# A gated-scan block: softmax of the gates spread over ScalarE, VectorE and GpSimd, with the scan states in PSUM

## The chip, the cores and the metric

The kernel runs on one core of one Trainium2 chip. The metric is the device time of one launch in microseconds; several runs of the same kernel are taken and their median is given. A core has TensorE (PE, matrix products[...]), VectorE (DVE), ScalarE (ACT), GpSimd (POOL) and the DMA queues that SyncE (SP) and ACT issue to. Each engine works through its own instructions in a fixed order and waits on semaphores for the others.

## The reference

One block works on x of shape 8 x 512 x 128 (batch, time, width), all in fp32. The part around the change is the attention half: a softmax over 17 values for each of 8 x 16 rows of each token, and a recurrence over time with these gates.

```python
h = _rmsnorm(x, norm_w)
v = (h @ W_v.T).reshape(B, T, H, M)                       # H = 8, M = 16
gate_logits = (h @ W_a.T).reshape(B, T, H, M, M + 1)
gates = jax.nn.softmax(gate_logits, axis=-1)
a0 = gates[..., 0]
A = gates[..., 1:]
A_t = jnp.moveaxis(A, 1, 0)
u_t = jnp.moveaxis(a0 * v, 1, 0)

def step(state, inp):
    At, ut = inp
    new = jnp.einsum('bhij,bhj->bhi', At, state) + ut
    return (new, new)
...
return x + h_out @ W_out.T
```

Before it stands a layernorm with modulation; after it a second one, a router that keeps 4 of 8 experts, and all 8 experts (128 to 256 gated, and back to 128) with their weighted sum.

## The kernel before

Tokens are taken in tiles of 128: 16 time steps of 8 batches. There are 32 tiles, and four of them make a superchunk. The scan is serial over all 32 tiles. The work is written as Python generators that yield where other work may come between; beside the scan of tile c run the output of the attention of tile c - 1 (`attn_out`), the gates of tile c + 2 (`gates`), and a quarter of the experts of the superchunk before (`experts`), with the first layernorm (`ln1`) or the second one and the router (`attn_post`) where they fall due. From this the framework makes the fixed order of each engine and all semaphores. The timeline shows that the order on an engine isn't simply the order of the text: pieces of two tiles' gates, scan steps and expert work are mixed, and the experts of a whole superchunk come in one stretch.

`gates(c)` (L203 to L248): ACT scales the normalised tokens, PE transposes them into a buffer of `ps_misc` (ph, L209), ACT copies them out (hnT, L211). PE then makes the 2176 logits of each token in five pieces, one PSUM bank each (pg, L220), in a pool of two banks; the last bank also holds v. For each piece DVE takes the maxima over 17 values (mx, L224) and subtracts them (ee, L226), and ACT takes the exponential (L229). Over the whole tile DVE then sums (z, L234), inverts (L235), scales (L238) and multiplies gate 0 by v (L241). Eight DMAs on SP's queue (L243) bring the tile from tokens-by-partition to g, which has the 64 pairs of head and batch on its partitions and time within them.

`scan(c)` (L250 to L262): for each of 16 time steps DVE multiplies the gates by the previous state (L256) and reduces over 17 values to the new state (L259), which lies in ys.

`attn_out(c)` (L264 to L282): eight DMAs on SP's queue bring ys back to tokens (yt, L269); PE transposes (py, L273), ACT copies (ytT, L275), PE multiplies by the output weights (po, L277), and DVE adds h (r, L281). py, po and ph, and the matrices of the second layernorm, the router and the experts' biases, all use buffers of `ps_misc`, of which there are two:

```python
ps_gate = ctx.enter_context(tc.tile_pool(name="ps_gate", bufs=2, space=PS))
ps_gu = ctx.enter_context(tc.tile_pool(name="ps_gu", bufs=3, space=PS))
ps_dn = ctx.enter_context(tc.tile_pool(name="ps_dn", bufs=1, space=PS))
ps_misc = ctx.enter_context(tc.tile_pool(name="ps_misc", bufs=2, space=PS))
```

The second layernorm's and router's lines are L287, L288, L174, L178, L179 and L320 to L329 on DVE. In the experts DVE's lines are L382 to L384 on the activations and L399 on the weighted sum; ACT's are L371, L373 and L375.

Of the kernel before, what the change touches and what calls it, by code (L numbers as in the profile page):

```python
# [9 lines left out]
F32 = mybir.dt.float32  # L10
AF = mybir.ActivationFunctionType
ALU = mybir.AluOpType
AX = mybir.AxisListType

P = 128
# [13 lines left out]
def adaln_block_kernel(  # L29
    ctx: ExitStack,  # L30
    tc: tile.TileContext,
    x: bass.AP,        # [B, T, D]
    norm_w: bass.AP,   # [D, 1]
    wa_t: bass.AP,     # [D, H*M*(M+1)]
    wv_t: bass.AP,     # [D, D]
    wo_t: bass.AP,     # [D, D]
    rw_t: bass.AP,     # [D, E]
    r_bias: bass.AP,   # [1, E]
    gu_t: bass.AP,     # [D, E*2I]
    gu_bias: bass.AP,  # [128, E*4]  # L40
    dn_t: bass.AP,     # [E, I, D]
    dn_bias: bass.AP,  # [E, D]
    c_in: bass.AP,     # [B, D]
    w_mod: bass.AP,    # [D, 6*D]
    out: bass.AP,      # [B, T, D]
):
    nc = tc.nc
    B, T, D = x.shape
    H, M = 8, 16
    J = M + 1               # softmax width  # L50
    NG = H * M              # softmax groups per token
    TT = P // B             # time steps in a tile of 128 tokens
    NT = T // TT            # tiles
    KT = 4                  # tiles in a superchunk
    NS = NT // KT
    E = rw_t.shape[1]
    I = dn_t.shape[1]
    IC = I // P
    NW = KT * P
    # (first softmax group, groups) of each PSUM bank; v goes into the last bank  # L60
    CHUNKS = [(0, 27), (27, 27), (54, 26), (80, 26), (106, 22)]

    const = ctx.enter_context(tc.tile_pool(name="const", bufs=1))
# [2 lines left out]
    scan_p = ctx.enter_context(tc.tile_pool(name="scan", bufs=3))  # L66
    ffn_p = ctx.enter_context(tc.tile_pool(name="ffn", bufs=3))
    small = ctx.enter_context(tc.tile_pool(name="small", bufs=2))
    PS = bass.MemoryType.PSUM
    ps_gate = ctx.enter_context(tc.tile_pool(name="ps_gate", bufs=2, space=PS))  # L70
    ps_gu = ctx.enter_context(tc.tile_pool(name="ps_gu", bufs=3, space=PS))
    ps_dn = ctx.enter_context(tc.tile_pool(name="ps_dn", bufs=1, space=PS))
    ps_misc = ctx.enter_context(tc.tile_pool(name="ps_misc", bufs=2, space=PS))

    def misc_psum(name):
        return ps_misc.tile([P, 512], F32, tag="misc", name=name)

# [1 line left out]
    c_sb = const.tile([B, D], F32, name="c_sb")  # L79
    nc.sync.dma_start(c_sb, c_in)  # L80
    wmod_sb = const.tile([P, 6 * D], F32, name="wmod_sb")
    nc.scalar.dma_start(wmod_sb, w_mod)
    x_sb = const.tile([P, NT, D], F32, name="x_sb")

    def load_x(c):
        nc.sync.dma_start(x_sb[:, c, :], x[:, c * TT : (c + 1) * TT, :])

    for c in range(KT):
        load_x(c)
    wav = const.tile([P, NG * J + D], F32, name="wav")  # L90
    nc.scalar.dma_start(wav[:, : NG * J], wa_t)
    nc.scalar.dma_start(wav[:, NG * J :], wv_t)
    nw_sb = const.tile([P, 1], F32, name="nw_sb")
    nc.sync.dma_start(nw_sb, norm_w)
    wo_sb = const.tile([P, D], F32, name="wo_sb")
    nc.sync.dma_start(wo_sb, wo_t)
    for c in range(KT, NT):
        load_x(c)
# [10 lines left out]
    dn_sb = const.tile([P, E * IC, D], F32, name="dn_sb")  # L109
    nc.scalar.dma_start(dn_sb, dn_t.rearrange("e (ic p) d -> p (e ic) d", p=P))  # L110

# [1 line left out]
    ident = const.tile([P, P], F32, name="ident")  # L113
    make_identity(nc, ident)
    eps_sb = const.tile([P, 1], F32, name="eps_sb")
    nc.gpsimd.memset(eps_sb, EPS)
    state0 = const.tile([H * B, M], F32, name="state0")
    nc.gpsimd.memset(state0, 0.0)
    # lower[e, f] = 1 where f < e: among equal logits the lower index goes first
    lower = const.tile([P, E, E], F32, name="lower")  # L120
    nc.gpsimd.memset(lower, 1.0)
    nc.gpsimd.affine_select(
        out=lower, in_=lower, compare_op=ALU.is_gt, fill=0.0, base=0,
        pattern=[[1, E], [-1, E]], channel_multiplier=0,
    )
    # up's bias with the 1 of (up + 1)
    ub1_sb = const.tile([P, E, IC], F32, name="ub1_sb")
    nc.vector.tensor_scalar(ub1_sb, gub_sb[:, :, IC:], 1.0, None, ALU.add)

# [1 line left out]
    sig_c = const.tile([B, D], F32, name="sig_c")  # L131
    nc.scalar.activation(sig_c, c_sb, AF.Sigmoid)
    sil = const.tile([B, D], F32, name="sil")
# [2 lines left out]
    nc.tensor.transpose(psil[:, :B], sil, ident[:B, :B])  # L136
    silT = const.tile([P, B, TT], F32, name="silT")
    nc.vector.tensor_copy(silT, psil[:, :B].unsqueeze(2).to_broadcast([P, B, TT]))
    mod = const.tile([P, 6, D], F32, name="mod")
# [18 lines left out]
    def mod_row(i):  # L158
        return mod[:, i, :].unsqueeze(1).to_broadcast([P, KT, D])

# [1 line left out]
    def layernorm(dst, src, scale_i, shift_i, tag):  # L162
        mv = small.tile([P, KT, 2], F32, tag="mv" + tag, name="mv" + tag)
        for k in range(KT):
# [13 lines left out]
        nc.vector.tensor_tensor(dst, dst, mod_row(scale_i), ALU.mult)  # L178
        nc.vector.tensor_tensor(dst, dst, mod_row(shift_i), ALU.add)  # L179

    # the parts below are generators: they yield where other work may come between
    h_tiles = {}      # superchunk -> (h, rms factor)
    g_tiles = {}      # tile -> gates for the scan
    y_tiles = {}      # tile -> scan states
    r_tiles = {}      # superchunk -> h + attention
    f_tiles = {}      # superchunk -> what the experts need

    def ln1(s):
        h = sc_p.tile([P, KT, D], F32, tag="h", name=f"h{s}", bufs=3)
# [13 lines left out]
    def gates(c):  # L203
        h, rr = h_tiles[c // KT]
        k = c % KT
        hn = tile_p.tile([P, D], F32, tag="hn", name=f"hn{c}")
        nc.scalar.activation(hn, h[:, k, :], AF.Copy, scale=rr[:, k : k + 1])
        ph = misc_psum(f"ph{c}")
        nc.tensor.transpose(ph[:, :P], hn, ident)  # L209
        hnT = tile_p.tile([P, P], F32, tag="hnT", name=f"hnT{c}")  # L210
        nc.scalar.activation(hnT, ph[:, :P], AF.Copy, scale=nw_sb)  # L211
        ee = tile_p.tile([P, NG, J], F32, tag="ee", name=f"ee{c}")
        mx = tile_p.tile([P, NG], F32, tag="mx", name=f"mx{c}")
        v = tile_p.tile([P, NG], F32, tag="v", name=f"v{c}")
        yield
        for g0, n in CHUNKS:
            last = g0 + n == NG
            w = n * J + (D if last else 0)
            pg = ps_gate.tile([P, 512], F32, tag="pg", name=f"pg{c}_{g0}")
            nc.tensor.matmul(  # L220
                pg[:, :w], hnT, wav[:, g0 * J : g0 * J + w], start=True, stop=True
            )
            pg3 = pg[:, : n * J].rearrange("p (g j) -> p g j", j=J)
            nc.vector.tensor_reduce(mx[:, g0 : g0 + n], pg3, AX.X, ALU.max)  # L224
            e3 = ee[:, g0 : g0 + n, :]
            nc.vector.tensor_tensor(  # L226
                e3, pg3, mx[:, g0 : g0 + n].unsqueeze(2).to_broadcast([P, n, J]), ALU.subtract
            )
            nc.scalar.activation(e3, e3, AF.Exp)  # L229
            if last:  # L230
                nc.scalar.copy(v, pg[:, n * J : w])
            yield
        z = tile_p.tile([P, NG], F32, tag="z", name=f"z{c}")
        nc.vector.tensor_reduce(z, ee, AX.X, ALU.add)  # L234
        nc.vector.reciprocal(z, z)  # L235
        yield
        g = scan_p.tile([H * B, TT, M, J], F32, tag="g", name=f"g{c}")
        nc.vector.tensor_tensor(  # L238
            ee, ee, z.unsqueeze(2).to_broadcast([P, NG, J]), ALU.mult
        )  # L240
        nc.vector.tensor_tensor(ee[:, :, 0], ee[:, :, 0], v, ALU.mult)  # L241
        for hh in range(H):
            nc.sync.dma_start(  # L243
                g[hh * B : (hh + 1) * B].rearrange("b t i j -> b t (i j)"),
                ee[:, hh * M : (hh + 1) * M, :].rearrange("p i j -> p (i j)"),
            )
        g_tiles[c] = g
        yield  # L248

    def scan(c):  # L250
        g = g_tiles.pop(c)
        ys = scan_p.tile([H * B, TT, M], F32, tag="ys", name=f"ys{c}")
        prev = state0 if c == 0 else y_tiles[c - 1][:, TT - 1, :]
        for t in range(TT):
            a = g[:, t, :, 1:]
            nc.vector.tensor_tensor(  # L256
                a, a, prev.unsqueeze(1).to_broadcast([H * B, M, M]), ALU.mult
            )
            nc.vector.tensor_reduce(ys[:, t, :], g[:, t, :, :], AX.X, ALU.add)  # L259
            prev = ys[:, t, :]  # L260
            yield
        y_tiles[c] = ys  # L262

    def attn_out(c):  # L264
        s, k = c // KT, c % KT
# [18 lines left out]
    def attn_post(s):  # L284
# [9 lines left out]
        h2T = sc_p.tile([P, NW], F32, tag="h2T", name=f"h2T_{s}")  # L294
        nc.scalar.copy(h2T, ph)
        yield
        # router: top 4 of 8, softmax over the chosen
        pr = misc_psum(f"pr{s}")
        for k in range(KT):
            nc.tensor.matmul(  # L300
# [16 lines left out]
        other = lg.unsqueeze(2).to_broadcast([P, KT, E, E])  # L317
# [21 lines left out]
            comb, comb, cs.unsqueeze(2).to_broadcast([P, KT, E]), ALU.mult  # L339
        )  # L340
        yield
        # the experts' output biases, weighted
        pc = misc_psum(f"pc{s}")
        for k in range(KT):
            nc.tensor.transpose(pc[:E, k * P : (k + 1) * P], comb[:, k, :], ident)
# [13 lines left out]
    def experts(s, es):  # L359
# [18 lines left out]
        def back(e, ic, gt, up, sg):  # L378
            if ic == 0:
                acts[e] = ffn_p.tile([P, IC, NW], F32, tag="act", name=f"act{s}_{e}", bufs=2)  # L380
            # clip(up, -7, 7) + 1, min(gate, 7), sigmoid(1.702 min(gate, 7))
            nc.vector.tensor_scalar(up, up, 1.0 - LIMIT, 1.0 + LIMIT, ALU.max, ALU.min)  # L382
            nc.vector.scalar_tensor_tensor(up, gt, LIMIT, up, ALU.min, ALU.mult)  # L383
            nc.vector.scalar_tensor_tensor(acts[e][:, ic, :], sg, SIG_MAX, up, ALU.min, ALU.mult)  # L384
# [50 lines left out]
        for _ in gen:  # L435
            pass

    # ---- the pipeline: beside the scan of tile c run the gates of tile c + 2,
    # the output of tile c - 1 and a part of the experts of the superchunk before
    run(ln1(0))  # L440
    run(gates(0))
    run(gates(1))
    for c in range(NT):
        s, k = c // KT, c % KT
        beside = []
# [12 lines left out]
        other = chain(*beside)  # L458
# [3 lines left out]
        run(other)  # L462
    run(attn_out(NT - 1))
    run(attn_post(NS - 1))
# [42 lines left out]
```

## Time and profile before

| | |
|---|---|
| median of 3 runs | 1391.12 us (1390.35 to 1391.66) |
| profiled execution: its span, the only time that its page gives | 1390.6 us |
| VectorE busy | 1151.2 us, 83% |
| TensorE matmuls busy | 675.7 us, 49% |
| ScalarE busy | 462.8 us, 33% |
| GpSimd busy | 1.1 us |
| DMA g<-ee | 256 DMAs of 136 KB on SP's queue |
| DMA yt<-ys | 256 DMAs of 8 KB on SP's queue |

In a row of a group stand the line, the engine, the operation, what is written from what, the shapes and the count; then busy time in us and the mean of one in ns; then the engine's idle time just before these instructions and what ended most of it. In a timeline a row begins with its start and its length in us, and an idle time before it stands in brackets with what ended it. In a table by stage a row begins with the stretch and its length, followed by the busy us (and count of instructions) of PE, PE's weight loads, DVE, ACT and POOL, the granted TensorE clock, the DMA engines' busy share and GB/s. Work that overlaps is counted once in an engine's busy time.

### The profile page before, as it was taken

How to read it: one execution, taken by the hardware profiler on the slowest of the kernel's cores; microseconds unless marked ns; L12 is line 12 of the kernel's file. 1: busy time of each engine (PE TensorE's matmuls, PEld its weight loads, DVE VectorE, ACT ScalarE, POOL GpSimd, SP SyncE). 2: the span in 40 equal slices, each digit the busy share in tenths (PEclk: the TensorE clock that was granted, in tenths of full speed). 3: DMA queues.
4: the chain of work that ended last, by engine and by line, in shares of the span. 5: the costliest groups of instructions: out<-in, count | busy, mean ns of one | idle time of the engine just before them, and what ended most of it. 6: DMA issues, size and time to landing. Idle time of an engine off the chain costs nothing.

```text
span 1390.6 us, 9491 instructions
## 1 busy us (share of the span) xinstructions
PE 675.7 (49%) x2181; PEld 348.3 (25%) x2181; DVE 1151.2 (83%) x2533; ACT 462.8 (33%) x850; POOL 1.1 (0%) x10
## 2 busy tenths in 40 slices
PE   1415049531594237830496315942369414771077
PEld 0101015310262014510153102620135201440044
DVE  3889699996999799996989969897898978888366
ACT  2401037320382115610373203821146102541054
POOL 0000000000000000000000000000000000000000
PEclk9755568865697667965688656976569756795579
DMA  6251514024330325005140242303241041501200
GB/s 199 32 60 14 60 21 49 1 32 45 36 31 10 44 25 65 2 11 63 20 51 0 30 48 33 34 10 38 31 50 17 10 54 20 61 1 21 24 0 8
DMA packets 80248, 47.39 MB, mean 34 GB/s; under 512 B 38064, under 2 KB 79296, under 8 KB 79936
## 3 DMA queue, kind: packets, MB, share of 16 engines
q1 hardware_dynamic: 78640, 42.03, 25.8%
q10 hardware_dynamic: 1552, 4.75, 1.0%
q14 instruction: 38, 0.31, 0.1%
q8 instruction: 18, 0.29, 0.1%
HBM read 6.91 MB, written 2.10 MB: 6 GB/s over the span
## 4 chain that ended last, share of the span: by engine, by line
DVE 40%; PE 32%; DMA 21%; issue 2%; SPq 2%; ACT 2%; DVEq 0%; ACTq 0%
DMA g<-ee 15%; PE pgt L365 9%; PE pd L391 8%; DVE g L256 8%; PE pup L367 8%; DVE ys L259 7%; DVE mx L224 5%; DVE z L234 5%; DMA yt<-ys 4%; PE pg L220 4%; DVE ee L226 4%; DVE ee L238 3%; SPq L243 2%; DVE z L235 2%; DMA x_sb<-in_x_dram 1%
## 5 line engine op out<-in xcount | busy, mean ns | idle before, releaser
L256 DVE TENSOR_TENSOR g<-g,ys 64x256 f32<-64x256 f32 x511 | 211.2, 413 | 107.0 <-DMA g<-ee 60.1
L220 PE MATMUL pg<-wav,hnT 128*128 128x459 f32 (+2 forms) x320 | 221.6, 815 | 133.5 <-DVE ee L226 108.7
L259 DVE TENSOR_REDUCE ys<-g 64x16 f32<-64x272 f32 x512 | 217.1, 424 | 11.3
L273 PE MATMUL py<-ident,yt 128*128 128x128 f32 x32 | 13.7, 427 | 436.5 <-DMA yt<-ys 435.8
L275 ACT COPY ytT<-py 128x128 f32<-128x128 f32 x32 | 8.5, 266 | 513.1 <-PE py L273 513.1
L391 PE MATMUL pd<-dn_sb,act 128*128 128x128 f32 x1024 | 146.6, 291 | 29.8 <-DVE act L384 16.2
L391 PEld LDWEIGHTS pd<-dn_sb,act 128*128 128x128 f32 x1024 | 136.2, 201 | 91.3 <-DVE act L384 36.6
L229 ACT ACTIVATE ee<-ee 128x459 f32<-128x459 f32 (+2 forms) x160 | 89.1, 564 | 201.4 <-DVE ee L226 179.6
L365 PE MATMUL pgt<-h2T,gu_sb 128*128 128x512 f32 x256 | 145.9, 654 | 0.0
L367 PE MATMUL pup<-h2T,gu_sb 128*128 128x512 f32 x256 | 138.8, 625 | 0.0
L220 PEld LDWEIGHTS pg<-wav,hnT 128*128 128x128 f32 x320 | 68.9, 254 | 257.2 <-issue 163.1
L273 PEld LDWEIGHTS py<-ident,yt 128*128 128x128 f32 x32 | 6.2, 193 | 461.3 <-issue 302.2
L224 DVE TENSOR_REDUCE mx<-pg 128x27 f32<-128x459 f32 (+2 forms) x160 | 95.1, 594 | 13.5 <-PE pg L220 12.8
L373 ACT ACTIVATE up<-pup,ub_sb 128x512 f32<-128x512 f32 x128 | 86.8, 678 | 40.8 <-PE pup L367 40.8
L371 ACT ACTIVATE gate<-pgt,gub_sb 128x512 f32<-128x512 f32 x128 | 87.6, 684 | 24.7 <-PE pgt L365 24.2
L226 DVE TENSOR_TENSOR ee<-pg,mx 128x459 f32<-128x459 f32 (+2 forms) x160 | 95.2, 595 | 0.0
L384 DVE SCALAR_TENSOR_TENSOR act<-sg,up 128x512 f32<-128x512 f32 x128 | 88.1, 688 | 7.4 <-ACT sg L375 3.4
L383 DVE SCALAR_TENSOR_TENSOR up<-gate,up 128x512 f32<-128x512 f32 x128 | 88.0, 688 | 2.9
L399 DVE SCALAR_TENSOR_TENSOR y<-pd,comb,y 128x128 f32<-128x128 f32 x256 | 74.9, 342 | 14.2 <-PE pd L391 13.9
L375 ACT ACTIVATE sg<-gate 128x512 f32<-128x512 f32 x128 | 80.5, 629 | 2.5
L234 DVE TENSOR_REDUCE z<-ee 128x128 f32<-128x2176 f32 x32 | 76.8, 2400 | 0.5 <-ACT ee L229 0.5
L238 DVE TENSOR_TENSOR ee<-ee,z 128x2176 f32<-128x2176 f32 x32 | 76.9, 2404 | 0.0
(89 smaller groups left out, 599.1 us busy)
## 6 DMA issues: line engine op xcount, KB each, us to landing
g<-ee SPq DMA_DIRECT2D x256, 136.0 KB
yt<-ys SPq DMA_DIRECT2D x256, 8.0 KB
x_sb<-in_x_dram SPq DMA_DIRECT2D x32, 64.0 KB
gu_sb<-in_gu_t_dram ACTq DMA_DIRECT2D x1, 2048.0 KB
out_dram<-y SPq DMA_DIRECT2D x32, 64.0 KB
wav<-in_wa_t_dram ACTq DMA_DIRECT2D x1, 1088.0 KB
wmod_sb<-in_w_mod_dram ACTq DMA_DIRECT2D x1, 384.0 KB
wo_sb<-in_wo_t_dram SPq DMA_DIRECT2D x1, 64.0 KB
```

The costliest lines, as they stand in the source:

```text
L220: nc.tensor.matmul(pg[:, :w], hnT, wav[:, g0 * J : g0 * J + w], start=True, stop=True)
L224: nc.vector.tensor_reduce(mx[:, g0 : g0 + n], pg3, AX.X, ALU.max)
L226: nc.vector.tensor_tensor(e3, pg3, mx[:, g0 : g0 + n].unsqueeze(2).to_broadcast([P, n, J]), ALU.subtract)
L229: nc.scalar.activation(e3, e3, AF.Exp)
L234: nc.vector.tensor_reduce(z, ee, AX.X, ALU.add)
L238: nc.vector.tensor_tensor(ee, ee, z.unsqueeze(2).to_broadcast([P, NG, J]), ALU.mult)
L256: nc.vector.tensor_tensor(a, a, prev.unsqueeze(1).to_broadcast([H * B, M, M]), ALU.mult)
L259: nc.vector.tensor_reduce(ys[:, t, :], g[:, t, :, :], AX.X, ALU.add)
L365: nc.tensor.matmul(pgt, gu_sb[:, e, ic * P : (ic + 1) * P], h2T, start=True, stop=True)
L367: nc.tensor.matmul(pup, gu_sb[:, e, I + ic * P : I + (ic + 1) * P], h2T, start=True, stop=True)
L384: nc.vector.scalar_tensor_tensor(acts[e][:, ic, :], sg, SIG_MAX, up, ALU.min, ALU.mult)
L391: nc.tensor.matmul(pd[:, k, :], act[:, ic, k * P : (k + 1) * P], dn_sb[:, e * IC + ic, :], start=(ic == 0), stop=(ic == IC - 1),)
```

## The change

The logits of all five banks are copied to SBUF by ACT. DVE takes the maxima of the whole tile in one instruction, GpSimd subtracts them, ACT takes one exponential of the whole tile, DVE sums and inverts as before, and GpSimd scales and multiplies gate 0 by v. The scan writes its states into one PSUM bank, yp, in two halves that tiles use in turn, and reads the previous state from there; after a tile's scan ACT copies its states to SBUF, from where the DMAs take them as before. The bank comes from `ps_misc`, which keeps one buffer. Comments that the diff drops are left out here.

```diff
-    ps_misc = ctx.enter_context(tc.tile_pool(name="ps_misc", bufs=2, space=PS))
+    ps_misc = ctx.enter_context(tc.tile_pool(name="ps_misc", bufs=1, space=PS))
+    ps_y = ctx.enter_context(tc.tile_pool(name="ps_y", bufs=1, space=PS))
...
+    yp = ps_y.tile([H * B, 2, TT, M], F32, name="yp")
...
             pg3 = pg[:, : n * J].rearrange("p (g j) -> p g j", j=J)
-            nc.vector.tensor_reduce(mx[:, g0 : g0 + n], pg3, AX.X, ALU.max)
-            e3 = ee[:, g0 : g0 + n, :]
-            nc.vector.tensor_tensor(
-                e3, pg3, mx[:, g0 : g0 + n].unsqueeze(2).to_broadcast([P, n, J]), ALU.subtract
-            )
-            nc.scalar.activation(e3, e3, AF.Exp)
+            nc.scalar.copy(ee[:, g0 : g0 + n, :], pg3)
             if last:
                 nc.scalar.copy(v, pg[:, n * J : w])
             yield
+        nc.vector.tensor_reduce(mx, ee, AX.X, ALU.max)
+        yield
+        nc.gpsimd.tensor_tensor(
+            ee, ee, mx.unsqueeze(2).to_broadcast([P, NG, J]), ALU.subtract
+        )
+        yield
+        nc.scalar.activation(ee, ee, AF.Exp)
+        yield
         z = tile_p.tile([P, NG], F32, tag="z", name=f"z{c}")
         nc.vector.tensor_reduce(z, ee, AX.X, ALU.add)
         nc.vector.reciprocal(z, z)
         yield
         g = scan_p.tile([H * B, TT, M, J], F32, tag="g", name=f"g{c}")
-        nc.vector.tensor_tensor(
+        nc.gpsimd.tensor_tensor(
             ee, ee, z.unsqueeze(2).to_broadcast([P, NG, J]), ALU.mult
         )
-        nc.vector.tensor_tensor(ee[:, :, 0], ee[:, :, 0], v, ALU.mult)
+        nc.gpsimd.tensor_tensor(ee[:, :, 0], ee[:, :, 0], v, ALU.mult)
...
-        ys = scan_p.tile([H * B, TT, M], F32, tag="ys", name=f"ys{c}")
-        prev = state0 if c == 0 else y_tiles[c - 1][:, TT - 1, :]
+        ys = yp[:, c % 2, :, :]
+        prev = state0 if c == 0 else yp[:, (c - 1) % 2, TT - 1, :]
...
-        y_tiles[c] = ys
+        y_tiles[c] = scan_p.tile([H * B, TT, M], F32, tag="ys", name=f"ys{c}")
+        nc.scalar.copy(y_tiles[c], ys)
```

## The prediction

> **What bounds the kernel now.** I read the busy rows first, then the groups, then the timeline of VectorE (DVE) and of the SP queue over one superchunk, and last a table by stage. The page's rows for the groups that the change touches, and for the scan:
>
> ```profile
> span 1390.6 us, 9491 instructions
> ...
> PE 675.7 (49%) x2181; PEld 348.3 (25%) x2181; DVE 1151.2 (83%) x2533; ACT 462.8 (33%) x850; POOL 1.1 (0%) x10
> ...
> L256 DVE TENSOR_TENSOR g<-g,ys 64x256 f32<-64x256 f32 x511 | 211.2, 413 | 107.0 <-DMA g<-ee 60.1
> L220 PE MATMUL pg<-wav,hnT 128*128 128x459 f32 (+2 forms) x320 | 221.6, 815 | 133.5 <-DVE ee L226 108.7
> L259 DVE TENSOR_REDUCE ys<-g 64x16 f32<-64x272 f32 x512 | 217.1, 424 | 11.3
> ...
> L234 DVE TENSOR_REDUCE z<-ee 128x128 f32<-128x2176 f32 x32 | 76.8, 2400 | 0.5 <-ACT ee L229 0.5
> L238 DVE TENSOR_TENSOR ee<-ee,z 128x2176 f32<-128x2176 f32 x32 | 76.9, 2404 | 0.0
> ```
>
> DVE is busy 83% of the span and POOL not at all. That alone would make any work taken off DVE a gain, so the next view asks whether DVE sets the pace everywhere. The first line of each pair of tiles is the addition of attention to h (r, L281). It starts at 116.8, 180.0, 281.3, 343.9, 445.2, 505.1, 605.5, 668.3, 769.6, 832.8, 933.5, 996.1, 1098.5, 1160.9 and 1262.4 us. So stages of about 63 and 101 us alternate: seven short, seven long. The table by stage, with a short one, the long one after it, and the short one of the first superchunk, where there are no experts yet:
>
> ```profile
> 771.00:834.00 63.00, 16.83 (x28) 6.10 (x27) 48.30 (x95) 8.99 (x19) 0.00 (x0) 0.58 0.36 41
> 834.00:935.00 101.00, 65.68 (x246) 36.91 (x245) 93.29 (x213) 47.11 (x85) 0.00 (x0) 0.82 0.22 24
> 118.00:182.00 64.00, 18.06 (x29) 6.61 (x28) 49.18 (x97) 7.82 (x18) 0.00 (x0) 0.55 0.34 37
> ```
>
> The third busy column is DVE. The long stage holds the experts and DVE is full (93 of 101 us). The short stage has DVE idle 14.7 of 63 us. What sets its length is a loop through two queues, seen in the timeline:
>
> ```profile
> 769.60 0.28 DVE L281 TENSOR_TENSOR r<-po,h 128x128 f32<-128x128 f32 x1
> ...
> 787.62 0.37 DVE L241 TENSOR_TENSOR ee<-ee,v 128x128 f32<-128x128 f32 x1
> ...
> 800.18 0.38 DVE L241 TENSOR_TENSOR ee<-ee,v 128x128 f32<-128x128 f32 x1
> 809.00 0.42 DVE L256 TENSOR_TENSOR g<-g,ys 64x256 f32<-64x256 f32 x1 [8.44 <-DMA g<-ee]
> ...
> 826.95 0.42 DVE L256 TENSOR_TENSOR g<-g,ys 64x256 f32<-64x256 f32 x1 [3.37 <-DMA yt<-ys]
> ...
> 832.77 0.28 DVE L281 TENSOR_TENSOR r<-po,h 128x128 f32<-128x128 f32 x1
> ```
>
> From r to the first tile's finished gates 18.4 us (769.6 to 788.0); the gate transfers of both tiles 38.9 us, one behind the other on SP's queue (788.0 to 826.9), the second tile being ready at 800.6, long before the first has landed; then the yt transfers that stand behind them, PE's py and po, and r again (5.9 us). The sum is the 63 us. In the short stage, then, the latency of the first tile's gates counts and DVE's load doesn't; in the long one it is the reverse.
>
> [...] L224 takes 610 ns for 459 elements out of PSUM and L234 2400 for 2176 out of SBUF[...].
>
> **The change part by part.**
>
> *DVE.* Per tile it loses the subtraction (95.2/32 = 2.98 us), the scaling (2.40) and the product with v (12.0/32 = 0.37), and the maximum goes from five pieces (95.1/32 = 2.97) to one of the size of z (2.40): 6.32 us, 202 us in all. In the long stages this is on the path: two tiles, -12.6 us each. In the short ones it only adds to DVE's idle time.
>
> *First tile's latency.* After: a transpose 0.4 (L209) and its ACT copy 0.4 (L211); PE's five banks 221.6/32 = 6.9, then the last ACT copy 0.5; maximum 2.4; subtraction on POOL; exp; sum 2.4 and reciprocal 0.9; scaling on POOL; product with v 0.4 (DVE's time, as estimate). [...] Exp of 2176: the rows give 584 ns for 459 and 511 for 374, hence 0.86 ns per element and an estimate of 2.1 us. Eight handoffs at about 0.15 (0.27 from exp to z at 780.3) add 1.2. Sum 27.2 us, against 18.4: **+8.8 us**. That PE's banks start only after r comes from the halved ps_misc: ph needs the buffer that po holds until r has read it. Before, ph went into the second buffer, and its first two matmuls ran at 754.8 while r came at 769.6. If the order on DVE puts r early, ACT empties the banks early, and only 1.5 us remain: these are the two bounds. The second tile's gates (maximum some 7 us later, POOL shared) end about 8 us after the first's, still inside its 21 us of transfer, so they cost nothing; the transfer is the cover.
>
> *ACT.* Copies of 587 ns for 512 (L295) and 247 for 128 (L231) give 0.54 for 459 columns: 2.6 us per tile for five; one exp of 2.1 in place of five (89.1/32 = 2.8); the states' copy 0.36. Sum +2.3 per tile, 73 us in all, ACT at 38%. Off the path, but two waits are new. [...] And the states' copy stands between a scan's last step and both its eight yt DMAs on SP and the next scan's first step (same bank): 0.36 plus handoffs, about 0.6. On the yt path that is +0.6 per stage; between scans it lies beside a wait for g in the short stage and costs up to 1.2 in the long. SP's issues (8 for g, 8 for yt, each 0.6) are the same in number; g's now wait for POOL.
>
> *POOL's lock.* [...]
>
> *Scan in PSUM.* Reads cost nothing more by the rows above. Writes by DVE to PSUM have no row[...]; I take 0, as for reads.
>
> *Start and end.* The gates of tile 0 come 6 us later (their DVE part was 15.5 us long between layernorm pieces, from 35.5 to 51.0; after it is about 21), those of tile 2, alone in their stage, 9 later, and so do those of tile 31 (the scan waits for them at 1300). The tail, from 1331 on, is experts alone and doesn't move.
>
> *Sum.* Short stages 7 x (8.8 + 0.6) = +66; long 7 x (-12.6 + 5 + 1.2) = -45; start and end +24: +45 on a span of 1390.6, which is 0.5 below the median shown. Rounded up for ps_misc in the router's chain, **1440 us**, slower by 3.5%.
>
> **The rivals.** *Faster: DVE's load decides everywhere.* If r comes early on DVE and POOL's pieces fall beside scan steps, short stages gain 1.5 us and long ones lose 12.6: 7 x (-11.1) + 15 = -63, 1328 us. For it: 14.7 idle us in short stages and POOL's empty row. Against: r, py and ph form one chain. It decides from the point where the latency growth of a short stage is below what a long stage saves net of the lock. At the far end all of DVE's 202 us would go (1190), which the short stages exclude. *Much slower: DVE waits inside its own order.* If z stands in DVE's order right behind the maximum, DVE waits for POOL and exp[...], and scan steps queue behind it. In the short stages idle time covers it; in the long it adds 14 x 7 = 98: 1538 us. For it: the order of issue is fixed and today carries 0.5 us of such waits. Against: independent work may stand between. *The lock costs its bound:* [...] *Nothing moves:* the seven losses and gains cancel; the gap between -45 and +66 makes that a narrow case.
>
> **How the numbers follow.** The forecast 0.43 (1400 to 1480), the two slower rivals 0.20 together, faster 0.33, no change 0.04. About 0.2% is what a measurement of this kernel can tell from none. The range goes from 1310[...] to 1540 (the stall or the lock in full); beyond each end lies about a tenth. The forecast's own range is 1400 to 1480.
>
> **What would show it.** Right: [...] short stages of 70 to 73 us with DVE idle over 25, still ended by g and yt transfers; long stages of 92 to 97. Wrong: short stages still 63, or stages that no longer alternate (faster); z or the maximum with several us of wait each on POOL or exp (stall); L383 and L384 with means well above 688 ns (lock); L256 or L259 above 430 ns (PSUM).

## The result and the profile after

| | before | after |
|---|---|---|
| median | 1391.39 us (1390.35 to 1393.91, 4 runs) | 1464.04 us (1461.84 to 1466.67, 4 runs) |
| ratio, 95% interval | | 1.052 [1.0503, 1.0536] |
| span of the profiled execution | 1390.6 us | 1460.1 us |

The change makes the kernel 5.2% slower; 3.5% was forecast. The page of the kernel after, busy times and the groups that answer to those shown of before (line, engine, operation, out<-in, shapes, count, then total busy us and mean ns, then the idle time before them and what ended it):

```profile
span 1460.1 us, 9224 instructions
...
PE 676.1 (46%) x2181; PEld 362.5 (25%) x2181; DVE 1082.5 (74%) x2181; ACT 528.7 (36%) x915; POOL 269.8 (18%) x106
...
L234 POOL TENSOR_TENSOR ee<-ee,mx 128x2176 f32<-128x2176 f32 x32 | 125.2, 3914 | 856.0 <-DVE mx L232 759.2
L263 DVE TENSOR_TENSOR g<-g,yp 64x256 f32<-64x256 f32 x511 | 209.0, 409 | 95.0 <-DMA g<-ee 44.3
...
L266 DVE TENSOR_REDUCE yp<-g 64x16 f32<-64x272 f32 x512 | 222.2, 434 | 15.0
...
L245 POOL TENSOR_TENSOR ee<-ee,z 128x2176 f32<-128x2176 f32 x32 | 125.3, 3917 | 198.9 <-DVE z L242 141.5
```

VectorE's share has fallen from 83 to 74% and GpSimd now works 270 us, but the span has grown by 69.5. Two things are to be seen. The scan's rows (L263, L266) cost what they cost with the states in SBUF, 409 and 434 ns against 413 and 424. And VectorE's busy time has dropped by 69 us only, where three passes and part of the maxima, 202 us in all, were taken off it. Adding up all of VectorE's rows gives 1251 us before and 1133 after: 118 less, because rows that have nothing to do with the gates have become longer by about 82. The other 50 us are how busy time is counted: VectorE's records overlap one another, and the busy line counts overlapped time once. The overlap was 1251 - 1151 = 100 us and is now 1133 - 1082 = 50. TensorE's matmuls are busy as long as before, 676.1 us against 675.7, so they aren't where the time went.

Rows that became longer, from the groups by shape; first two of before, then those of after (L382 and L312 of before are L390 and L320 of after):

```profile
L382 DVE TENSOR_SCALAR up<-up 128x512 f32<-128x512 f32 x128 | 54.2, 423 | 21.3 <-ACT up L373 20.3
L312 DVE TENSOR_TENSOR le<-lg,lmx 128x32 f32<-128x32 f32 x8 | 1.5, 188 | 0.0
```

```profile
L390 DVE TENSOR_SCALAR up<-up 128x512 f32<-128x512 f32 x128 | 72.3, 567 | 35.2 <-ACT up L381 34.8
L391 DVE SCALAR_TENSOR_TENSOR up<-gate,up 128x512 f32<-128x512 f32 x128 | 94.5, 742 | 2.9
L392 DVE SCALAR_TENSOR_TENSOR act<-sg,up 128x512 f32<-128x512 f32 x128 | 93.8, 736 | 8.6 <-ACT sg L383 4.9
L175 DVE TENSOR_SCALAR h<-x,mvb,rstdb 128x128 f32<-128x128 f32 x32 | 25.9, 862 | 0.1
L320 DVE TENSOR_TENSOR le<-lg,lmx 128x32 f32<-128x32 f32 x8 | 16.3, 2032 | 0.0
```

Before, these took 423, 688, 688, 334 and 188 ns. The mean of 2032 ns mixes two cases. Of the eight instructions of L320 four take 0.18 us as before, and four take 3.88 us. Each of these four starts just after one of GpSimd's scalings and ends with it. One of them, first VectorE's row, then GpSimd's:

```profile
942.78 3.88 DVE L320 TENSOR_TENSOR le<-lg,lmx 128x32 f32<-128x32 f32 x1
```

```profile
942.64 3.98 POOL L245 TENSOR_TENSOR ee<-ee,z 128x2176 f32<-128x2176 f32 x1 [8.35 <-DVE lmx L318]
```

So these instructions are held until GpSimd's is done. In all, 34 of VectorE's instructions are more than 0.2 us longer than is usual for their kind, together by 84 us, and each of them runs while a GpSimd instruction does. In the kernel before there is none.

VectorE's waits, after (line waited at, what it waited for, us in total, times, longest). Before, the maxima waited 12.8 us in all, and the sum z for ScalarE's exponentials 0.5:

```profile
DVE g L263 <- DMA g<-ee: 64.3, 5, 20.0
DVE z L241 <- ACT ee L238: 50.4, 20, 4.2
DVE up L390 <- ACT up L381: 34.8, 74, 1.9
DVE mx L232 <- ACT ee L228: 32.9, 21, 5.2
DVE r L289 <- PE po L285: 31.5, 10, 8.8
```

The sum z now stands behind ScalarE's exponential of the whole tile, which stands behind GpSimd's subtraction; the maximum stands behind five copies; and r behind po, where po, py and ph now share one buffer. VectorE's time adds up: it is busy 69 us less and idle 138 us more (378 against 239), which makes the 69.5 us of the span. The waits for z, the maxima, r and up, and the one at L407 for PE's pd (30.6 us, 13.9 before), make 124 of the 138. This is bookkeeping on one engine; it doesn't say which wait would be worth removing.

The latency of a tile's gates, from the timeline after (start in us, length in us, engine, line; in brackets the idle time before it and its releaser). VectorE first, then GpSimd:

```profile
824.78 0.27 DVE L289 TENSOR_TENSOR r<-po,h 128x128 f32<-128x128 f32 x1
...
833.58 2.42 DVE L232 TENSOR_REDUCE mx<-ee 128x128 f32<-128x2176 f32 x1 [2.69 <-ACT ee L228]
...
842.05 2.42 DVE L241 TENSOR_REDUCE z<-ee 128x128 f32<-128x2176 f32 x1 [2.76 <-ACT ee L238]
```

```profile
836.08 3.89 POOL L234 TENSOR_TENSOR ee<-ee,mx 128x2176 f32<-128x2176 f32 x1 [37.67 <-DVE mx L232]
845.60 3.89 POOL L245 TENSOR_TENSOR ee<-ee,z 128x2176 f32<-128x2176 f32 x1 [5.63 <-DVE z L242]
849.57 0.52 POOL L248 TENSOR_TENSOR ee<-ee,v 128x128 f32<-128x128 f32 x1
```

From r to the finished gates it takes 25.3 us (824.8 to 850.1), where it took 18.4 before. This is one of the quick cases. From r to the finished gates of three tiles later, as here, tiles 12 to 19 take 28, 42, 29, 31, 25, 29, 85 and 25 us, where all tiles before took 17 to 29. In the one of 85 us, ScalarE's copies of all five banks stand behind the experts of a superchunk (736 to 777 us). The stages no longer alternate between 63 and 101 us; a pattern over eight tiles repeats instead. Two superchunks, after (the stretch, then its length and the busy us of PE, PE's loads, VectorE, ScalarE and GpSimd):

```profile
348.00:696.00 348.00, 168.96 (x544) 90.47 (x544) 268.53 (x541) 131.78 (x228) 66.96 (x24) 0.70 0.25 29
696.00:1044.00 348.00, 171.28 (x544) 92.11 (x544) 268.98 (x525) 129.32 (x224) 67.33 (x24) 0.70 0.25 29
```

The same work took 324 to 329 us before, with VectorE busy for 283. The first line r of tile 0 comes 14.4 us later than before (131.2 against 116.8), that of tile 8 31.3, of tile 16 55.2, of tile 24 71.4 and of tile 31 68.8. So after a start of 14 the loss grows by about 9 us per superchunk up to tile 24, and not after that.

### The profile page after: what moved, and what is told of

Read it like the earlier page. It is cut to its first block, busy times and chain, and to the rows that moved or that the text cites. A ratio compares the mean times of both kernels' runs of the same rounds, so it can differ in the third digit from the quotient of the medians.

```text
span 1460.1 us, 9224 instructions
## 1 busy us (share of the span) xinstructions
PE 676.1 (46%) x2181; PEld 362.5 (25%) x2181; DVE 1082.5 (74%) x2181; ACT 528.7 (36%) x915; POOL 269.8 (18%) x106
## 4 chain that ended last, share of the span: by engine, by line
DVE 33%; PE 29%; DMA 17%; POOL 7%; ACT 6%; issue 4%; SPq 4%; ACTq 0%; DVEq 0%; POOLq 0%
DMA g<-ee 10%; PE pd L399 7%; PE pg L224 7%; DVE yp L266 6%; PE pup L375 6%; PE pgt L373 6%; DMA yt<-ys 6%; DVE g L263 6%; DVE z L241 4%; DVE mx L232 3%; POOL ee L234 3%; POOL ee L245 3%; DVE h L175 3%; SPq L250 2%; ACT ee L238 2%
## 5 line engine op out<-in xcount | busy, mean ns | idle before, releaser
L234 POOL TENSOR_TENSOR ee<-ee,mx 128x2176 f32<-128x2176 f32 x32 | 125.2, 3914 | 856.0 <-DVE mx L232 759.2
L263 DVE TENSOR_TENSOR g<-g,yp 64x256 f32<-64x256 f32 x511 | 209.0, 409 | 95.0 <-DMA g<-ee 44.3
L224 PE MATMUL pg<-wav,hnT 128*128 128x459 f32 (+2 forms) x320 | 202.3, 785 | 131.0 <-ACT ee L228 95.1
L266 DVE TENSOR_REDUCE yp<-g 64x16 f32<-64x272 f32 x512 | 222.2, 434 | 15.0
L399 PE MATMUL pd<-dn_sb,act 128*128 128x128 f32 x1024 | 152.1, 297 | 49.5 <-DVE act L392 34.0
L245 POOL TENSOR_TENSOR ee<-ee,z 128x2176 f32<-128x2176 f32 x32 | 125.3, 3917 | 198.9 <-DVE z L242 141.5
L228 ACT COPY ee<-pg 128x459 f32<-128x459 f32 (+2 forms) x160 | 81.0, 521 | 165.3 <-PE pg L224 87.0
L270 ACT COPY ys<-yp 64x256 f32<-64x256 f32 x32 | 11.7, 364 | 296.7 <-DVE yp L266 296.7
L241 DVE TENSOR_REDUCE z<-ee 128x128 f32<-128x2176 f32 x32 | 77.2, 2414 | 50.4 <-ACT ee L238 50.4
L232 DVE TENSOR_REDUCE mx<-ee 128x128 f32<-128x2176 f32 x32 | 77.3, 2415 | 34.2 <-ACT ee L228 32.9
L392 DVE SCALAR_TENSOR_TENSOR act<-sg,up 128x512 f32<-128x512 f32 x128 | 93.8, 736 | 8.6 <-ACT sg L383 4.9
L390 DVE TENSOR_SCALAR up<-up 128x512 f32<-128x512 f32 x128 | 72.3, 567 | 35.2 <-ACT up L381 34.8
L238 ACT ACTIVATE ee<-ee 128x2176 f32<-128x2176 f32 x32 | 64.5, 2017 | 93.0 <-POOL ee L234 92.9
L407 DVE SCALAR_TENSOR_TENSOR y<-pd,comb,y 128x128 f32<-128x128 f32 x256 | 73.2, 341 | 30.8 <-PE pd L399 30.6
```

The costliest lines, as they stand in the source:

```text
L224: nc.tensor.matmul(pg[:, :w], hnT, wav[:, g0 * J : g0 * J + w], start=True, stop=True)
L232: nc.vector.tensor_reduce(mx, ee, AX.X, ALU.max)
L234: nc.gpsimd.tensor_tensor(ee, ee, mx.unsqueeze(2).to_broadcast([P, NG, J]), ALU.subtract)
L245: nc.gpsimd.tensor_tensor(ee, ee, z.unsqueeze(2).to_broadcast([P, NG, J]), ALU.mult)
L263: nc.vector.tensor_tensor(a, a, prev.unsqueeze(1).to_broadcast([H * B, M, M]), ALU.mult)
L399: nc.tensor.matmul(pd[:, k, :], act[:, ic, k * P : (k + 1) * P], dn_sb[:, e * IC + ic, :], start=(ic == 0), stop=(ic == IC - 1),)
```

## The experiments

Times are medians; the ratio is to the kernel before on the same chip. The names of lines are those of the kernel after unless said otherwise. One warning holds for all of them. The framework makes a new order for each kernel: of the pairs set side by side here only `misc1` and `copy_sbuf` have the same order of VectorE's instructions from the first to the last. To turn the order of the kernel before into that of `misc1`, at least 345 of 2533 instructions have to be moved; for `piece_max` it is 553 of 2373. From the kernel after to `pool_writes` it is 208 of 2181, to `sbuf_scan` 262, to `no_sub` 494 and to `dve_softmax` 506. So a difference in time between two kernels is the worth of the edit together with that of the order that it brings.

**1. Buffers alone: `misc1`, the kernel before with one buffer in ps_misc.**

```diff
-    ps_misc = ctx.enter_context(tc.tile_pool(name="ps_misc", bufs=2, space=PS))
+    ps_misc = ctx.enter_context(tc.tile_pool(name="ps_misc", bufs=1, space=PS))
```

> The kernel before with one buffer in ps_misc instead of two, nothing else. Theory of the latency (the trips over POOL and ACT lengthen the first tile's gates where transfers set the pace): small, 0 to +1%, since in the kernel before the first two banks of logits stood ready 15 us before VectorE took them. Theory of PSUM (the halved ps_misc and the states' bank cost the time): +2% or more. Theory of the lock (VectorE's instructions wait for GpSimd's): 0.

1415.11 us, 1.0176 [1.0161, 1.0191], between the two ranges. This line alone, with the order that it brings, costs 25 us, a third as much as the whole change. The short stages stay near 63 us, the long ones go from 101 to 103. VectorE waits at r for PE's po 17.1 us (16 times) where it waited 8.3 (once). My prediction counted the halved pool only as part of the latency of the first tile.

**2. States in PSUM: `psum_scan`, `misc1` with the states in a PSUM bank and ScalarE's copy, the softmax as before.**

```diff
+    ps_y = ctx.enter_context(tc.tile_pool(name="ps_y", bufs=1, space=PS))
...
+    yp = ps_y.tile([H * B, 2, TT, M], F32, name="yp")
...
-        ys = scan_p.tile([H * B, TT, M], F32, tag="ys", name=f"ys{c}")
-        prev = state0 if c == 0 else y_tiles[c - 1][:, TT - 1, :]
+        ys = yp[:, c % 2, :, :]
+        prev = state0 if c == 0 else yp[:, (c - 1) % 2, TT - 1, :]
...
-        y_tiles[c] = ys
+        y_tiles[c] = scan_p.tile([H * B, TT, M], F32, tag="ys", name=f"ys{c}")
+        nc.scalar.copy(y_tiles[c], ys)
```

> The kernel before with only the second part of the change: states in PSUM, ScalarE's copy of them, one buffer in ps_misc; the softmax as before. Theory of the latency: 0 to +1.5% (the copy adds some 0.5 us between two scans, at most 16 us in all). Theory of PSUM: +4 to +5%, all of the loss. Theory of the lock: 0 to +1%.

1438.38 us, 1.0343 [1.0314, 1.0372]: 23 us more than `misc1`, and between the ranges of the first two theories. The two scan rows are 408 and 432 ns (413 and 424 before), so access to PSUM is not what costs. What does? Two kernels take it apart.

`copy_sbuf` has the same two-half tile and the same copy, with the tile in SBUF:

```diff
...
-    yp = ps_y.tile([H * B, 2, TT, M], F32, name="yp")
+    yp = const.tile([H * B, 2, TT, M], F32, name="yp")
```

> The kernel before with one buffer in ps_misc, and the scan's states in one SBUF tile of two halves from which ScalarE copies each tile's states, as the change does from PSUM. It tells apart what the second part of the change costs beyond the halved ps_misc (psum_scan 1438 us against misc1 1415). If the copy itself costs it (yt's transfers leave later, and each waits for ScalarE): 1430 to 1440. If it is [...]: 1413 to 1420.

1417.77 us, 1.0189 [1.0171, 1.0208]: the copy costs 3 us over `misc1`, with VectorE's order the same, and the PSUM bank 21. It lies in the second range, where my guess was that the copy and the scan meeting in one bank cost it; this run doesn't show that, and the next kernel takes the meeting away.

`psum_dve` is `psum_scan` with the copy on VectorE, so that no two engines meet on the bank:

```diff
-        nc.scalar.copy(y_tiles[c], ys)
+        nc.vector.tensor_copy(y_tiles[c], ys)
```

> The kernel before with ps_misc halved and the states in a PSUM bank, as psum_scan, but the copy of a tile's 64x256 states to SBUF is made by VectorE instead of ScalarE, so no engine but VectorE touches that bank and no scan step waits for ScalarE. psum_scan took 1438, the same with the states in SBUF (copy_sbuf) 1418. If the cost of about 20 us is the ordering of VectorE and ScalarE on one bank: 1418 to 1428, of which 32 copies of about 0.35 us are 11 at most. If it is the place of the copy in VectorE's and ScalarE's fixed order of work, or PSUM itself: 1435 to 1450, and VectorE's waits at the maxima (46 us in psum_scan against 13) stay above 35.

1442.52 us, 1.0355 [1.0329, 1.038]. The 20 us do not go away, so the meeting of two engines on one bank is not their cause. VectorE's waits at the maxima, 46.4 us in `psum_scan` and 54.3 here against 12.7 in `copy_sbuf`, point to the place. The timeline of VectorE in `psum_scan`, where the maxima are L226 and the subtractions L228:

```profile
801.40 0.64 DVE L226 TENSOR_REDUCE mx<-pg 128x27 f32<-128x459 f32 x1 [0.29 <-PE pg L222]
802.93 0.64 DVE L226 TENSOR_REDUCE mx<-pg 128x27 f32<-128x459 f32 x1 [0.89 <-PE pg L222]
803.48 1.17 DVE L228 TENSOR_TENSOR ee<-pg,mx 128x459 f32<-128x459 f32 x2
...
806.11 0.62 DVE L226 TENSOR_REDUCE mx<-pg 128x26 f32<-128x442 f32 x1 [0.94 <-PE pg L222]
```

And the same place in `copy_sbuf` (maxima L225, subtractions L227):

```profile
790.94 0.64 DVE L225 TENSOR_REDUCE mx<-pg 128x27 f32<-128x459 f32 x1 [0.30 <-PE pg L221]
...
791.84 0.62 DVE L227 TENSOR_TENSOR ee<-pg,mx 128x459 f32<-128x459 f32 x1
792.47 0.64 DVE L225 TENSOR_REDUCE mx<-pg 128x27 f32<-128x459 f32 x1
```

A subtraction is what frees a bank, and the pool has two. In `copy_sbuf` the order on VectorE is maximum, subtraction, maximum, subtraction; the bank is free while the next maximum runs, and PE keeps ahead. In `psum_scan` two maxima stand before the subtractions (x2 is two records in one), both banks are held, and each next maximum waits 0.9 us for PE. From the first maximum to z a tile takes 11.2 us (801.4 to 812.6) instead of 8.8 (790.9 to 799.7). Over all 32 tiles this stretch adds up to 408.7 us in `psum_scan` and 385.3 in `copy_sbuf`, 23 us more, and a maximum stands before the subtraction of the piece ahead of it at 31 of 128 places against 1. So the traces put the 21 us down to another fixed order of VectorE, made by the framework, and show nothing that PSUM itself costs beyond some 4 us of the row that writes the states (432 ns against 424, 512 times). It is a reading of the traces; a kernel with PSUM states and the old order was not run. In the kernel after, ScalarE's copies free the banks, so this term does not carry over.

**3. The softmax without GpSimd: `dve_softmax`, the kernel after with GpSimd's three operations on VectorE.**

```diff
-        nc.gpsimd.tensor_tensor(      # L234, L245, L248
+        nc.vector.tensor_tensor(
```

> The changed kernel with its three GpSimd instructions per tile on VectorE, all else as changed. VectorE gets back 5.2 us a tile (166 us), the chain of a tile's gates loses 2 x (3.9 - 2.4) us and four handoffs, and no lock is left. Theory of the latency: 1430 to 1470 us, short stages shorter and long ones longer. Theory of the lock: 1385 to 1410, the 82 us by which VectorE's instructions grew come back. Theory of PSUM: 1450 to 1500.

1518.26 us, 1.0912 [1.0886, 1.0938], and 54 us more than the kernel after. This lies outside the ranges of all three theories. VectorE is busy 1159.0 us and waits 119 us for g at the scan; L390 to L392 are back at 425, 688 and 689 ns, so the longer rows come with GpSimd: none of VectorE's instructions is held here, and yet the kernel is slower. In these two kernels GpSimd's part is a gain of 54, its holding of VectorE included, so by these runs it isn't what makes the change lose. The rest of the change is left for that: the buffers, copies by ScalarE and passes over the whole tile, and the order. Against `psum_scan`, which shares the buffers and the PSUM states and has the softmax in pieces out of PSUM, it is 80 us slower.

**4. States back in SBUF under GpSimd: `sbuf_scan`, the kernel after with the scan of before and two buffers in ps_misc.**

```diff
+    ps_misc = ctx.enter_context(tc.tile_pool(name="ps_misc", bufs=2, space=PS))
...
-        ys = yp[:, c % 2, :, :]
+        ys = scan_p.tile([H * B, TT, M], F32, tag="ys", name=f"ys{c}")
...
```

> The changed kernel with its states back in SBUF and two buffers in ps_misc; the softmax as changed. Theory of the latency: -1 to +1% against the changed kernel. Theory of the lock: +2 to +5%, because the scan's multiply now has two SBUF inputs and waits for GpSimd too, and its mean rises well above 409 ns. Theory of PSUM: back to 1390 to 1410 us.

1498.53 us, 1.0778 [1.0761, 1.0794]: 34 us slower than after, although ps_misc has its second buffer back, and within the range of the lock. The scan's multiplication, from the page of `sbuf_scan`:

```profile
L261 DVE TENSOR_TENSOR g<-g,ys 64x256 f32<-64x256 f32 x511 | 291.5, 570 | 116.3 <-DMA g<-ee 77.0
```

With both inputs in SBUF the mean goes from 409 to 570 ns, 82 us in sum. Again it mixes two cases: 23 of the 511 take 3.5 to 4.1 us, and the middle one takes 416 ns. With the state in PSUM none of them is held: in the kernel after 70 of the multiplications run from start to end beside a GpSimd instruction, and the longest of all takes 418 ns. In these kernels the PSUM half of the change earns its place once GpSimd works, and not before.

**5. The reads of GpSimd: `pool_writes` and `no_sub`.** `pool_writes` keeps GpSimd busy for as long, but with fills, which read nothing (only the small product with v, 0.55 us a tile, still reads). `no_sub` leaves out one of its two large operations.

```diff
-        nc.gpsimd.tensor_tensor(ee, ee, mx..., ALU.subtract)
+        for _ in range(2):
+            nc.gpsimd.memset(ee, 0.0)     # pool_writes; L245 likewise
```

> The changed kernel with each of GpSimd's two large instructions replaced by two fills of the same tile with a constant, which read nothing (the softmax is left out; the waits before and after stay). Two fills should take 3.6 to 4 us, as one instruction does. Theory of the lock: 1385 to 1430, L391, L392, L320 and L295 back at their means of before. Theory of the latency: 1440 to 1470.

1418.12 us, 1.0196 [1.0174, 1.0217]: 46 us less than after, with GpSimd as long busy (264 us) and z waiting for it as before (56.7 us for the exponential). It lies in the range of the lock. The group rows of `pool_writes`:

```profile
L390 DVE SCALAR_TENSOR_TENSOR act<-sg,up 128x512 f32<-128x512 f32 x128 | 87.2, 688 | 7.7 <-ACT sg L381 3.8
...
L388 DVE TENSOR_SCALAR up<-up 128x512 f32<-128x512 f32 x128 | 65.5, 517 | 26.6 <-ACT up L379 26.3
```

The experts' operations with two SBUF inputs are back at their old length or within 10 ns of it (688 and 698 ns), and the router's is 184 ns again, 2032 after. The operations with one tensor input and scalars (L388 with 517 ns, and the layernorm's with 1085 and 757) are still long: single ones of them take up to 2.0 us, about as long as a fill of 1.93. Two of the eight of L294, which has two SBUF inputs, take 1.64 us (0.68 else); they begin 0.26 us after such a long one of the layernorm and end with it. Two of the router's L344 take 0.50 us instead of 0.19. So the meeting of VectorE and GpSimd has two kinds here, and what fills leave is mostly the second. VectorE is held for 31 us in sum, where it was 84 after (overlaps counted once): 53 less, and the kernel is 46 us faster. So the reads can account for the 46 us, and the handoffs are in this number on both sides; but VectorE's order isn't quite the same, and the number isn't proved to be the price of the reads.

```diff
-        nc.gpsimd.tensor_tensor(ee, ee, mx..., ALU.subtract)     # no_sub
```

> The changed kernel without GpSimd's subtraction: the exponential takes the logits as they are (the maxima are still taken, but not used). The chain of a tile's gates loses 3.9 us and a handoff[...]. Theory of the latency: -30 us (7 short stages, and the start) to -45, hence 1420 to 1435. Theory of the lock: half of 82 us, 1420 to 1430 as well, but then L390, L175 and L320 lose half of their growth. Theory that VectorE's own order decides: within 15 us of the changed kernel.

1417.92 us, 1.0192 [1.0172, 1.0212]: 46 us less too, 2 us under the ranges of the latency and of the lock. VectorE is held for 34 us. The run takes away half of the meetings (L390's equal goes to 481 ns, the router's to 1109) and about 4 us of latency per tile at once; it doesn't tell the two apart, `pool_writes` does in part.

**6. The copies and passes in pieces: `pieces`, the kernel after with maximum, subtraction and exponential on each bank's part of ee.**

```diff
-            nc.scalar.copy(ee[:, g0 : g0 + n, :], pg3)
+            nc.scalar.copy(e3, pg3)
+            nc.vector.tensor_reduce(mx[:, g0 : g0 + n], e3, AX.X, ALU.max)
+            nc.gpsimd.tensor_tensor(e3, e3, mx..., ALU.subtract)
+            nc.scalar.activation(e3, e3, AF.Exp)
...
-        nc.vector.tensor_reduce(mx, ee, AX.X, ALU.max)
-        nc.gpsimd.tensor_tensor(ee, ee, mx..., ALU.subtract)
-        nc.scalar.activation(ee, ee, AF.Exp)
```

> The changed kernel with maxima, subtraction and exponential by the piece of a PSUM bank again (VectorE from SBUF, GpSimd, ScalarE), so that they run beside the matmuls of the next piece; scaling stays whole on GpSimd. The chain behind the last bank loses 1.8 us on VectorE, 3 on GpSimd and 1.5 on ScalarE. Theory of the whole tile (the serial passes over 2176 columns lengthen the chain): 1400 to 1430. Theory of the lock: no better than the changed kernel, 1455 to 1480[...].

1494.81 us, 1.075 [1.073, 1.077], 31 us slower than after. A miss: with the passes overlapped piece by piece I thought the latency would shrink. GpSimd is busy 292 us instead of 270, VectorE waits at the maxima 91 times (50.5 us) and at z 49.5 us. It is held for 27 us only, 57 less than after, so less holding doesn't by itself make a kernel faster. That the whole-tile form is the reason for the loss of 80 us in experiment 3 is not borne out; each of these kernels also gets its own order, and the question stays open.

**7. VectorE's work taken off with nothing put in its place: `piece_max`.** It is the kernel before with one maximum per token and bank, which the exponential takes as its bias: no subtraction, 95 us less for VectorE, no GpSimd, no copies, all buffers as before.

```diff
-            nc.vector.tensor_reduce(mx[:, g0 : g0 + n], pg3, AX.X, ALU.max)
-            nc.vector.tensor_tensor(e3, pg3, mx..., ALU.subtract)
-            nc.scalar.activation(e3, e3, AF.Exp)
+            nc.vector.tensor_reduce(nm, pg[:, : n * J], AX.X, ALU.max, negate=True)
+            nc.scalar.activation(ee[:, g0 : g0 + n, :], pg3, AF.Exp, bias=nm)
```

> The kernel before with no subtraction at all: VectorE takes one negated maximum per token and PSUM bank, and ScalarE's exponential reads the bank and adds it as its bias. A softmax doesn't change with a shift common to its 17 values, so the result is the same; states in SBUF, two buffers in ps_misc, GpSimd unused. VectorE loses 95 us, the chain gets shorter by a piece's subtraction (0.6 us) and ScalarE's exponential grows by some 0.1 us a piece. Theory of the latency and of VectorE's load together: long stages -6 us, short ones -1 to -4: 1320 to 1350. If the order of issue spoils it: 1370 to 1400.

1392.23 us, 1.001 [1.0003, 1.0017]: nothing gained, with VectorE at 1078.4 us instead of 1151.2. This is the range that was put down for an order of issue that spoils it. The table by stage of `piece_max`, a short stage and a long one:

```profile
769.44:833.32 63.88, 14.89 (x26) 5.98 (x27) 44.99 (x89) 8.17 (x18) 0.00 (x0) 0.55 0.36 41
833.32:934.88 101.56, 67.50 (x247) 37.92 (x245) 89.04 (x203) 49.21 (x86) 0.00 (x0) 0.80 0.22 24
```

The long stage is 101.6 us as before, with VectorE 4 us less busy. Two things are seen in the traces. The first appears when the long stage of the kernel before is cut at the experts:

```profile
834.00:862.00 28.00, 12.59 (x25) 4.29 (x24) 27.87 (x53) 9.60 (x18) 0.00 (x0) 0.74 0.22 26
862.00:905.00 43.00, 42.32 (x176) 25.79 (x176) 37.75 (x94) 32.70 (x59) 0.00 (x0) 0.91 0.36 37
```

VectorE is full for the first 28 us, but for the next 43 TensorE is (42.3 us), with the matmuls of the experts one behind the other. The second is the order. In `piece_max` the first tile's gates end at 850.8 (850.1 before) and the second's at 858.7, 6.5 us earlier than before (865.2). But VectorE's new order then puts the layernorm of the next superchunk (L174, L178 and L179, from 858.9 to 865.9) before the router, where it stood behind it, and the first matmul of the experts starts at 867.1 instead of 864.6. VectorE's first work for them starts at 871.5 (869.8 before), and it waits for ScalarE more often (at up 37.1 us in the whole kernel, 95 times, against 20.3, 58 times). So being busy for 93 of 101 us did not make VectorE the bound of the whole stage, and what it gained in the part where it is full, the new order gave away. What the lighter VectorE would be worth in the old order is not shown.

**8. The loop through SP's queue: `yt_pool` (before) and `after_yt` (after) with the yt DMAs on another queue.**

```diff
-            nc.sync.dma_start(yt[:, hh * M : (hh + 1) * M], ys[hh * B : (hh + 1) * B])
+            nc.gpsimd.dma_start(...)      # yt_pool; after_yt: nc.scalar.dma_start(...)
```

> The kernel before with the yt transfers issued on GpSimd's idle queue instead of SP's. A test of the loop through SP's queue: if yt's place behind the gate transfers sets the length of the short stages, they fall from 63 us to VectorE's 48 us or little above: 7 x 10 to 15 us, 1285 to 1325. If the transfers of g alone, or the order on VectorE, set it, nothing moves: 1380 to 1400.

> The changed kernel with the yt transfers issued on ScalarE's queue instead of SP's (GpSimd's is in use). If the loop through SP's queue is what makes the longer chain of the gates count, this gives back most of the loss against the kernel before: 1370 to 1410. If waits on ScalarE for a scan's end hold back what is queued there: 1450 to 1500.

1770.36 us, 1.2732 [1.2699, 1.2764], and 1723.45 us, 1.2389 [1.2368, 1.241]. Both miss by far. The largest waits of VectorE are at r for po, 397.0 and 429.2 us: the tiles no longer come in pairs but one at a time, 43 to 71 us from r to r in `yt_pool`. VectorE's fixed order is another: at least 937 of its 2533 instructions stand elsewhere. The runs say nothing on the loop as I read it; they say how much one DMA's queue moves the order of everything else.

## Why the prediction was right or wrong

*Right.* Slower, and the time lies in the range. The growth of a tile's latency was put at 8.8 us and is 6.9 in the tile shown (25.3 against 18.4). GpSimd's operation, twice in a tile, is 3.91 us; the 8.8 had more for it, an estimate of mine that nothing before showed, and that is most of the difference. The exponential is 2.02 us against an estimated 2.1, the copies 0.54 us as estimated, and only GpSimd's product with v, 0.58, is longer. The scan in PSUM costs next to nothing: a step from 804.33 to 805.25, 0.92 us, against 0.92 before. Reading costs nothing more: a maximum over 459 elements takes 610 ns out of PSUM before and 626 out of SBUF in `pieces`. The row that writes the states went from 424 to 434 ns, just over the 430 that the prediction had set as a sign, which makes 5 us in 512 steps. ScalarE's copy of the states takes 0.36 us as put down, and the scan waits for it 13 times, 5.6 us in all.

*In part luck.* The sum counts seven short and seven long stages, which the kernel after doesn't have, and its errors run in both directions. That it came within 25 us is no proof of its terms.

*Wrong: "long 7 x (-12.6 ...)".* The step that failed is "in the long stages this is on the path", said of the whole stage. It took a busy share of 93 in 101 us for a bound. The cut in experiment 7 shows VectorE full for 28 of the 101 us and TensorE for 43. `piece_max` takes 95 us of work off VectorE, some 6 in a long stage; the stage keeps its 101 us and the kernel gains nothing, though its order is another. Without the -88 us of this term, the prediction's own sum would be +133, and the measured +69.5 lies between. Some other term must then have been too large; the +66 of the short stages is the one at hand, but their growth cannot be read off singly, since the stages of the kernel after don't map to those of before. That is left open.

*Mis-sized: the lock.* That GpSimd's instructions would hold VectorE's, and for how long, was my estimate; nothing before showed it. I took 5 us per long stage, 35 in all, from three meetings, each for half of a GpSimd instruction. Measured, a meeting adds 2.5 us on average: half of them add over 3 us, up to 3.7, nearly a whole GpSimd instruction of 3.9, and the rest less. There are 34 of them instead of 21, 84 us in sum, in the router's rows, both layernorms', the experts' and that of the last modulation (L435). `pool_writes` and `no_sub`, with some 50 us less of holding each, are 46 us faster. A read of GpSimd's is not needed for every kind of meeting: the fills of `pool_writes`, which read nothing, hold the layernorm's operations with one tensor input (334 to 1085 ns).

*Left out: the PSUM buffers.* ps_misc with one buffer costs 25 us in the kernel before (`misc1`, its order included), for which the prediction had a few us of rounding. In the kernel after VectorE waits at r for po 31.5 us (10 times), 8.3 before.

*The rivals.* VectorE waiting in its own order came about in part: z and the maximum wait 50.4 and 32.9 us, where 98, with my estimate for GpSimd in it, was the price if every wait of a long stage counted. "Stages that no longer alternate" was to mean faster; they don't alternate, and it is slower. At the start 6 and 9 us were put down for the gates of tiles 0 and 2; these end 10.3 and 17.0 us later, and the first r comes 14.4 us later. The tail holds: from the last r to the end it is 67.6 us before and 68.3 after.

*Where the time went, as runs side by side.* From 1390 to 1415 with one buffer in ps_misc, to 1438 with the states in PSUM, to 1518 with copies and whole-tile passes on VectorE, and back to 1464 with GpSimd. These are whole kernels, each in its own order, and the steps aren't terms of a sum: the second one works through an order that the kernel after doesn't have. As kernels stand here, GpSimd's help is worth 54 us, doing without one of its two large operations or without its reads 46 more, and PSUM states 34 beside it. What the trace of the kernel after shows is VectorE held for 84 us and idle for 138 us more, most of it behind z, the maxima and r. Not shown is why the softmax through copies and whole tiles costs 80 us against the one that reads PSUM directly (1518 against 1438): its longer chain and its order were not told apart, and doing it in pieces didn't help. None of the kernels here is faster than the one before; `piece_max` comes within 0.1% of it.

## What to carry to other kernels

A high busy share in a stage need not be a bound (93 of 101 us here): before pricing work taken off an engine, cut the stage into parts and see which engine is full in each, or run a kernel that takes the work away and puts nothing in its place. Price a new GpSimd pass twice, once as latency in the chain (3.91 us for 128x2176 here) and once by the VectorE rows that can meet it, of the kinds that were held here: with two SBUF inputs, or with one tensor input and scalars (34 instructions, 84 us in sum). Look at single instructions, since a mean hides a few long ones (2032 ns from 0.18 and 3.88 us). Moving one operand to PSUM took the scan's row out of that here (570 ns to 409). Where a framework makes the fixed order of each engine, a change of one buffer, copy or queue changes the order too, so compare the orders before looking for a hardware cause.

## What was not expected of the hardware

GpSimd's elementwise pass over 128x2176 took 3.91 us, 1.63 times VectorE's 2.40, where my estimate, which nothing before showed, had a larger factor. Fills by GpSimd, which read nothing, still lengthened VectorE's one-input operations with scalars: 423 to 517 ns for 512 elements, and 334 to 1085 and 757 for the layernorm's 128, as means. In the kernel after a router instruction of 0.18 us took 3.88 when it met GpSimd's scaling, and 0.18 when it didn't.
